# Four graph-attention layers on one core: another engine order for the last blocks of two layers, and a residual addition moved from VectorE to TensorE and ScalarE

## The chip, the core and the metric

The kernel runs on one core of a Trainium2 chip. TensorE (PE, with its weight loads PEld), VectorE (DVE), ScalarE (ACT), GpSimd (POOL) and SyncE (SP) each work through a queue of their own, in order; semaphores hold an instruction until what it needs is done. Times are device microseconds (us) of one execution.

## The reference

4096 nodes with 256 features go through four attention layers over one sparse symmetric graph `adj` (about 9 neighbours to a node, itself among them). With `h = relu(layernorm(x))` each layer adds to the residual:

```
layer 0:  x += elu(softmax_over_neighbours(leaky(s_i + s_j)) @ Wh)        Wh = h W, 4 heads
layer 1:  x += h W + softmax_over_neighbours(leaky(s1_i + s2_j)) @ h      1 head
layer 2:  x += softmax_over_neighbours(leaky(s_i + s_j)) @ x',            x' = h W + b, 4 heads
layer 3:  x += softmax_over_neighbours(q k / 8) @ v                       4 heads
```

The text counts layers 0 to 3 as here; the change's "layers two and three" are layers 1 and 2.

## The kernel before

**Stages.** A scan reads the adjacency matrix, makes each node's list of up to 24 neighbours, sorts the nodes by degree into 32 blocks of 128, and does layer 0's first six neighbours of each node. Then `late` (L1122 to L1347) does what is left of layer 0 and makes layer 1's rows; `layer(1)`, `layer(2)` and `layer(3)` follow (L1349 to L1536). A block has between 3 and 23 slots for neighbours (`CAPS`), 15 of them at most are gathered one by one. For each slot GpSimd issues one indirect DMA (`fetch`, L1047, the call in L1048), which brings 128 rows, one per partition, from a table in DRAM into a ring in SBUF. The first gather of a layer needs every row of that layer's table, since any node may be anyone's neighbour.

**One block in a layer** passes through these stages, each a function inside `layer`:

- `scores` (L1538): the neighbours' scores on VectorE and ScalarE, and the exp on ScalarE; in layer 1 ScalarE adds the two halves of the score (L1550, L1551), and VectorE compares lists (L1608); in layer 2 VectorE adds them (L1553, L1554).
- `weigh` (L1615): VectorE makes the weights (L1627, L1628) and multiplies the gathered rows in the ring (L1654); TensorE sums the products over the slots with an identity matrix (L1634, L1662, L1668) in PSUM.
- `settle` (L1675): VectorE brings the new x out of PSUM (L1689) and takes its statistics (L960, L962); ScalarE turns them into scale and shift in a chain of eight tiny instructions (L965 to L972).
- `norm`: ScalarE makes h (L975), TensorE transposes it (L985).
- `flip`: ScalarE copies the transposed h to SBUF (L987).
- `product`: TensorE multiplies it with the next layer's weights (L1028).
- `third`: the product leaves PSUM, is stored to the next table by SP (L1712 in layer 1, L1730 in layer 2). In layer 1 ScalarE copies it (L1710), for the last two blocks VectorE adds the bias (L1708). In layer 2 VectorE adds biases to k and v (L1728) and q (L1732), then multiplies q with k and reduces (L1735, L1739), and ScalarE sums squares of q and k (L1742).

**What sets the order.** `manual_schedule` keeps the engines' instructions in program order, so the loop in `layer` is the order written out by hand. In step i it scores and weighs the i-th block of `ORDER`, and does the other stages for earlier blocks, by lags: S for settle, N for norm, Q for product, F for flip, T for third. `upto(name, k)` does a stage for all blocks up to k. Lags shrink over the last six steps. After the loop come the stages of what is left. TensorE's four PSUM banks are handed out by hand; `room` first does flips and thirds where too few are free. `told_by` makes a reader that comes in a later step than the product wait for the last sum of that step instead of for the product itself.

**The late part** goes over 19 groups of one or two blocks (`LATE`). `settle(i)` there is a generator of five steps: (0) ScalarE's exp of the sum, and minus 1 (L1287, L1288); (1) VectorE makes the new x (L1290, L1291) and its statistics; (2) scale and shift (L661 to L666), h on ScalarE (L1300), transposes on TensorE (L1307); (3) ScalarE copies them (L1310), and `times` (L1020) multiplies with layer 1's extended weights (L1028); (4) VectorE adds h W to x (L1317), ScalarE copies the scores' halves (L1318) and the list of neighbours (L1319) into the row, which GpSimd then sends to its place in the table (L1065). Each iteration does these for several groups:

```
scores(i)
go_on(i - 2)   # step 2
go_on(i - 1)   # step 0
go_on(i - 3)   # step 4
go_on(i - 2)   # step 3
weigh(i)
go_on(i - 1)   # step 1
```

Of the kernel before, what the change touches and what calls it, by code (L numbers as in the profile page):

```python
# [14 lines left out]
ALU = mybir.AluOpType  # L15
# [5 lines left out]
D = 256  # L21
# [30 lines left out]
W = 264  # L52
# [21 lines left out]
RAW = 6  # L74

AHEAD = 4

BOUND = 4900.0


class Sparse:
# [935 lines left out]
        self.wrote.append(m.ins)  # L1017
        self.latest = m.ins

    def times(self, ht, w, width, name, bias=None, ps=None):  # L1020
        if ps is None:
            ps = self.bank(f"s_ps_{name}")
        if bias is not None:
            self.writes(self.nc.tensor.matmul(
                ps[:, :width], lhsT=self.line, rhs=bias[0:1, :width], start=True, stop=False
            ))
        for c in range(KC):
            self.writes(self.nc.tensor.matmul(  # L1028
                ps[:, :width], lhsT=ht[:, c, :], rhs=w[:, c, :],
                start=(c == 0 and bias is None), stop=(c == KC - 1),  # L1030
            ))
        return ps[:, :width]

    def covered(self, g, start, size):
# [87 lines left out]
    def late(self):  # L1122


        nc, pool, nt, H = self.nc, self.pool, self.nt, 4
# [155 lines left out]
        def settle(i):  # L1281

            m, _ = size(i)
            xt, acc = part(i, 0, D), sums.pop(i)

            ex = pool.tile([P, 2, D], F32, name=f"s_ex_{i}", tag="ex", bufs=2)[:, :m, :]
            nc.scalar.activation(ex, acc, AF.Exp)  # L1287
            nc.scalar.activation(ex, ex, AF.Copy, bias=-1.0)  # L1288
            yield
            nc.vector.scalar_tensor_tensor(ex, ex, 0.0, xt, ALU.min, ALU.add)  # L1290
            nc.vector.scalar_tensor_tensor(xt, acc, 0.0, ex, ALU.max, ALU.add)  # L1291
            norm = self.norms_of(pool, xt if m > 1 else xt[:, 0, :], m, f"0_{i}", self.minus)
            for _ in range(m if m > 1 else 0):
                next(norm)
            next(norm)
            yield
            rn = next(norm)
            h = part(i, D, 2 * D)
            for u in range(m):
                nc.scalar.activation(  # L1300
                    h[:, u, :], xt[:, u, :], AF.Relu,
                    bias=rn[:, m + u : m + u + 1], scale=rn[:, u : u + 1],
                )
            pt = self.pp.tile([P, IB], F32, tag="ps", name=f"s_pht_0_{i}")
            for u in range(m):
                for c in range(KC):
                    nc.tensor.transpose(pt[:, ts(KC * u + c, P)], h[:, u, ts(c, P)], self.ident)  # L1307
            yield
            ht = pool.tile([P, 2, KC, P], F32, name=f"s_ht_0_{i}", tag="ht0", bufs=2)
            nc.scalar.copy(  # L1310
                ht[:, :m], pt[:, : m * KC * P].rearrange("p (n c r) -> p n c r", n=m, c=KC)
            )
            ps = [self.times(ht[:, u], self.we1, W, f"1_{i}_{u}") for u in range(m)]
            yield
            first = LATE[i][0]
            for u in range(m):
                nc.vector.tensor_tensor(xt[:, u, :], xt[:, u, :], ps[u][:, 0:D], ALU.add)  # L1317
                nc.scalar.copy(part(i, 2 * D, D + W)[:, u, :], ps[u][:, D:W])  # L1318
            nc.scalar.copy(part(i, D + W, D + WL), self.near[:, first : first + m, 0:TOPK])  # L1319
            pending.extend(LATE[i])  # L1320
            yield

# [26 lines left out]
    def layer(self, l):  # L1349
# [124 lines left out]
        def third(d):  # L1474
            if l < 3:
                step, wrote = when["row", d]
                self.reads = []
                next(rows.pop(d), None)
                if step < now:
                    for i in self.reads:  # L1480
                        told_by(i, wrote, step)
            while made and (len(made) > 1 or todo == []):
                i = self.send(*made.pop(0)).ins
                next_in_line(i)
                self.tc.declare_no_dep(i, group="results", reason="places differ")
                self.tc.add_to_no_dep_group("results", i)

        stages = {"settle": settle, "norm": norm, "flip": flip, "product": product, "third": third}
        done = {name: 0 for name in stages}

        def upto(name, k):
# [1 line left out]
                stages[name](ORDER[done[name]])  # L1493
                done[name] += 1

        for i in range(nt):
            now = i
            left = nt - 1 - i
            if l == 3:
                S = 1 if left < 3 else 2  # L1500
                N = F = Q = S + 1
                T = N
            else:
                S = 1 if left < 5 else 2
                N = 2 if left < 4 else 3
                Q = 2 if left < 2 else 3 if left < 4 else 4 if left < 6 else 5
                F, T = max(N, Q - 1), Q + 1
            fill(i)
            if (l, i) == (2, 4):
                self.symmetric()  # L1510
            b = ORDER[i]
            upto("norm", i - N)
            upto("product", i - Q)
            g = ring[:, held[b][0] : held[b][1], :]
            p = self.scores(l, b, self.rows[b], g)
            if l == 3:
                upto("third", i - T)
            sums[b] = self.weigh(l, b, vs.pop(b) if l == 3 else self.rows[b][:, 0:D], g, p)
            start, end = held.pop(b)
            past.append((start * wide, end * wide, self.read))  # L1520
            self.ever.append((start * wide, end * wide, self.read[0]))
            if l < 3:
                signals[i] = self.read[1]
            upto("settle", i - S)
            if l < 3:
                upto("flip", i - F)
                upto("third", i - T)
        now = nt
        upto("norm", nt - 2)
        upto("third", nt - 3)  # L1530
        upto("product", nt - 2)
        upto("settle", nt - 1)
        upto("norm", nt - 1)
        upto("third", nt - 2)
        upto("product", nt - 1)
        upto("third", nt - 1)  # L1536

    def scores(self, l, b, mine, g):  # L1538

# [155 lines left out]
    def advance(self, l, b, ht, made):  # L1695

        nc, pool = self.nc, self.pool
        xt = self.x[b]
        name = f"{l}_{b}"
        mine = self.rows[b]  # L1700
        if l == 2:
            short = b in ORDER[-2:]
            ps = self.times(ht, self.we2, W, name, None if short else self.be2)
            of_row = self.lent
            yield
            self.give(of_row)
            if short:
                i = nc.vector.tensor_tensor(mine, ps, self.be2, ALU.add)  # L1708
            else:
                i = nc.scalar.copy(mine, ps)  # L1710
            self.reads.append(i.ins)
            nc.sync.dma_start(out=self.tab[2][ts(b, P), :], in_=mine)  # L1712
        else:
            ps = self.times(ht, self.wkv, 2 * D, f"kv{name}")
            of_kv = self.lent
            spot, self.spot = self.spot, None
            if spot is not None and self.owed.get(spot[1]) == 1:
                of_q, spot = spot[1], spot[0]
# [9 lines left out]
            i = nc.vector.tensor_tensor(kv, ps, self.bqkv[:, D:], ALU.add)  # L1728
            self.reads.append(i.ins)
            nc.sync.dma_start(out=self.tab[3][ts(b, P), :], in_=kv)  # L1730
            q = mine[:, 0:D]
            i = nc.vector.tensor_tensor(q, ps_q, self.bqkv[:, 0:D], ALU.add)  # L1732
            self.reads.append(i.ins)
            qk = pool.tile([P, 4, 64], F32, name=f"s_qk_{b}", tag="qk", bufs=2)
            nc.vector.tensor_tensor(  # L1735
                qk, q.rearrange("p (h d) -> p h d", h=4),
                kv[:, 0:D].rearrange("p (h d) -> p h d", h=4), ALU.mult,
            )
            nc.vector.tensor_reduce(self.eself[:, b, :], qk, AX.X, ALU.add)  # L1739
            for k, v in ((0, q), (1, kv[:, 0:D])):  # L1740
# [580 lines left out]
```

## Time and profile before

| what | value |
|---|---|
| median of 15 runs | 1672.92 us (1665.64 to 1677.36) |
| profiled execution, its own time | 1673.05 us |
| its span, first to last instruction | 1671.3 us |
| granted TensorE clock, mean | 0.832 |
| busy: POOL, DVE, PE, ACT | 1142.2, 1109.1, 1078.3, 536.4 us |
| first gather of the late part, of layers 1, 2, 3 | 363.11, 543.06, 907.41, 1280.75 us |

A line of the timeline has the start, the duration, the engine and line, what it writes and reads with shapes, and in brackets how long the engine stood before it and what ended that. "issue" is time for which the profile shows no wait. A line of the waits has who waited for whom, the us in total, how often, and the longest. In a group's line of the page, the numbers behind the bar are busy us, the mean in ns, and the idle time before. A matrix product in 32-bit floats appears as two instructions.

### The profile page before, as it was taken

The page shows a single profiled execution, that of the slowest core. Times are in us where ns is not written, and L with a number is a line of the kernel's source. Part 1 is how long each engine was busy: PE and PEld are TensorE (multiplying, and loading weights), DVE is VectorE, ACT ScalarE, POOL GpSimd, SP SyncE. Part 2 cuts the span into 40 slices and gives each one's busy share as a digit, 9 for nine tenths or more (in the row PEclk, how much of TensorE's full clock was granted, in tenths as well). Part 3 has the DMA queues.
Part 4 walks back from the last instruction along what each step waited for, and adds up shares of the span by engine and source line. Part 5 has one row for each costly group of instructions (what it writes and reads, how often), then busy time and mean ns, then how long its engine had stood idle before and what let it go on. Part 6 is the DMA issues. An engine that isn't in the chain of part 4 may idle for free.

```text
span 1671.3 us, 14041 instructions
## 1 busy us (share of the span) xinstructions
PE 1078.3 (65%) x3179; PEld 584.6 (35%) x3179; DVE 1109.1 (66%) x2651; ACT 536.4 (32%) x1754; POOL 1142.2 (68%) x1241
## 2 busy tenths in 40 slices
PE   5857877605776357777784478778794455545555
PEld 4423333203443133444343234444452222322233
DVE  6669899816885255455552456676774797788787
ACT  6867664103344023333343023334342000000000
POOL 1267777767774777777772777777762777777775
PEclk9969989956897677898897689999998678777778
DMA  7899999466551444444442435444542776767664
GB/s 271 303 396 394 355 394 326 146 223 164 156 165 63 115 119 127 132 131 130 133 137 64 109 107 146 138 133 138 143 129 90 211 221 204 215 202 211 203 209 144
DMA packets 125908, 309.07 MB, mean 185 GB/s; under 512 B 35028, under 2 KB 53463, under 8 KB 125816
## 3 DMA queue, kind: packets, MB, share of 16 engines
q0 software_dynamic: 66832, 203.64, 41.8%
q1 hardware_dynamic: 58984, 104.46, 17.7%
q8 instruction: 27, 0.44, 0.1%
q14 instruction: 65, 0.53, 0.1%
HBM read 273.00 MB, written 35.00 MB: 184 GB/s over the span
## 4 chain that ended last, share of the span: by engine, by line
POOL 28%; DMA 22%; DVE 19%; issue 16%; ACT 9%; PE 6%; DVEq 0%; SPq 0%; POOLq 0%; ACTq 0%
POOL s_ring L1048 23%; DMA s_raw<-in_adj_dram 10%; DMA s_ring<-s_tab,s_near 10%; DVE s_ring L1654 5%; ACT s_low L277 2%; POOL s_placed L722 2%; POOL s_g L1048 1%; DVE s_ring L1575 1%; PE s_bank L1028 1%; DVE s_e L1579 1%; PE s_acc L1662 1%; POOL out_dram L1065 1%; DVE s_rx L1689 1%; DVE s_me L1639 1%; PE s_ps_t L1028 1%
## 5 line engine op out<-in xcount | busy, mean ns | idle before, releaser
L1048 POOL DMA_INDIRECT s_ring<-s_tab,s_near x900 | 855.7, 951 | 339.6 <-issue 266.6
L1662 PE MATMUL s_acc<-s_ring,s_ident 128*128 128x512 f32 (+1 forms) x1002 | 466.4, 623 | 273.3 <-DVE s_ring L1654 272.7
L1662 PEld LDWEIGHTS s_acc<-s_ring,s_ident 128*128 128x128 f32 x1002 | 225.5, 233 | 491.8 <-DVE s_ring L1654 305.0
L1048 POOL DMA_INDIRECT s_g<-s_tab,s_keep x192 | 182.8, 952 | 129.3 <-DMA s_raw<-in_adj_dram 65.5
L1654 DVE TENSOR_TENSOR s_ring<-s_ring,s_shares 128x2048 f32<-128x2048 f32 (+1 forms) x153 | 232.8, 1552 | 0.0
L277 ACT ACTIVATE s_low<-s_raw 128x1024 fp8e4<-128x1024 int32 x128 | 135.1, 1056 | 63.8 <-DMA s_raw<-in_adj_dram 62.3
L1600 ACT ACTIVATE s_shares<-s_e 128x40 f32<-128x40 f32 (+7 forms) x64 | 13.1, 205 | 332.4 <-DVE s_e L1597 332.4
L520 PE MATMUL s_pt<-s_low,s_mark_True 128*128 128x512 fp8e4 x256 | 83.6, 407 | 55.9 <-DVE s_cand L532 47.5
L1575 DVE TENSOR_TENSOR s_ring<-s_ring,s_shares 128x2048 f32<-128x2048 f32 (+7 forms) x47 | 78.8, 1676 | 55.9 <-DMA s_ring<-s_tab,s_near 38.8
L965 ACT ACTIVATE s_y<-s_mv,s_eps 128x1 f32<-128x1 f32 x64 | 18.8, 294 | 276.1 <-DVE s_mv L962 250.0
L532 DVE MAX8 s_cand<-s_pt 128x8 f32<-128x256 f32 x256 | 93.1, 415 | 13.8 <-PE s_pt L530 13.8
L1608 DVE TENSOR_SCALAR s_eq<-s_ring,s_own_f 128x207 bf16<-128x207 f32 (+12 forms) x32 | 12.5, 390 | 129.4 <-DMA s_ring<-s_tab,s_near 129.1
L631 PE MATMUL s_ae<-s_g,s_ident 128*128 128x512 f32 x192 | 90.8, 602 | 3.9 <-DVE s_g L622 3.9
L1579 DVE TENSOR_REDUCE s_e<-s_ring 128x32 f32<-128x2048 f32 (+7 forms) x47 | 78.9, 1679 | 1.6
L1028 PE MATMUL s_bank<-s_wkv,s_ht 128*128 128x512 f32 x128 | 62.9, 615 | 2.4 <-ACT s_ht L987 2.3
L520 PEld LDWEIGHTS <-s_mark_True 128*128 128x128 bf16 x256 | 23.3, 101 | 108.2 <-issue 61.4
L1028 PE MATMUL s_ps<-s_we_l,s_ht 128*128 128x264 f32 x128 | 45.0, 506 | 23.9 <-ACT s_ht L1310 23.9
L1634 PE MATMUL s_acc<-s_rx,s_ident 128*128 128x256 f32 x192 | 59.5, 393 | 0.0
L1307 PE MATMUL s_pht<-s_ident,s_rx 128*128 128x128 f32 x64 | 13.8, 325 | 69.1 <-DMA s_ring<-s_tab,s_near 50.8
L1668 PE MATMUL s_acc<-s_me,s_ident 128*128 128x256 f32 x192 | 57.1, 379 | 0.0
L622 DVE TENSOR_TENSOR s_g<-s_g,s_pe 128x1536 f32<-128x1536 f32 x32 | 55.4, 1735 | 0.0
L924 PE MATMUL s_bank<-s_to,s_to_row 128*128 128x32 f32 (+1 forms) x6 | 1.8, 393 | 81.4 <-DVE s_to L918 81.4
(286 smaller groups left out, 1830.6 us busy)
## 6 DMA issues: line engine op xcount, KB each, us to landing
s_raw<-in_adj_dram SPq DMA_DIRECT2D x128, 512.0 KB, 9.6
s_ring<-s_tab,s_near POOLq DMA_INDIRECT x900, 3.0
s_rx<-s_placed SPq DMA_DIRECT2D x32, 262.0 KB, 3.2
s_tab<-s_kv SPq DMA_DIRECT2D x32, 256.0 KB, 2.5
s_tab<-s_rx SPq DMA_DIRECT2D x32, 132.0 KB, 1.9
s_keep<-in_x_dram SPq DMA_DIRECT2D x8, 512.0 KB, 8.2
s_vself<-s_tab SPq DMA_DIRECT2D x32, 128.0 KB, 3.4
s_tab<-s_keep SPq DMA_DIRECT2D x7, 528.0 KB, 3.7
```

Of the source, the lines that this page charges most:

```text
L277: nc.scalar.activation(low[r][:, quarter(q)], raw.pop(q), AF.Copy, saturate=False, accum_out=self.sums[:, r, h : h + 1],)
L520: nc.tensor.matmul(pt, lhsT=self.mark[k], rhs=lo[:, k * PAIR + g * IB : k * PAIR + (g + 1) * IB], start=(k == 0), stop=False,)
L532: nc.vector.max(out=cand[:, g * (IB // CH) + k, :], in_=pt[:, ts(k, CH)])
L631: self.behind(got, nc.tensor.matmul(acc, lhsT=self.ident, rhs=g[:, :, k, 0:D], start=False, stop=(k == E - 1)))
L1028: self.writes(self.nc.tensor.matmul(ps[:, :width], lhsT=ht[:, c, :], rhs=w[:, c, :], start=(c == 0 and bias is None), stop=(c == KC - 1),))
L1048: return self.nc.gpsimd.indirect_dma_start(out=out, out_offset=None, in_=table[:, :], in_offset=bass.IndirectOffsetOnAxis(ap=idx, axis=0),)
L1575: scaled = nc.vector.tensor_tensor(kq, kq, q.unsqueeze(1).to_broadcast([P, m, D]), ALU.mult)
L1579: nc.vector.tensor_reduce(e[:, k0 : k0 + m, :], kq.rearrange("p k (h d) -> p k h d", h=4), AX.X, ALU.add)
L1634: self.took_x[b] = nc.tensor.matmul(acc[:, 1, :], lhsT=self.ident, rhs=self.x[b], start=True, stop=False)
L1654: scaled = nc.vector.tensor_tensor(v, v, p[:, k0 : k0 + m, :].unsqueeze(3).to_broadcast([P, m, H, D // H]), ALU.mult)
L1662: self.behind(self.got.get((l, b), ()), nc.tensor.matmul(acc[:, 0:n, :], lhsT=self.ident, rhs=g[:, k : k + n, v0 : v0 + D], start=False, s ...
L1668: last = nc.tensor.matmul(acc[:, 0, :], lhsT=self.ident, rhs=mev, start=False, stop=True).ins
```

## The change

Two edits that share nothing.

**The late part.** `times` gets an argument `also`: between the two halves of a row's product TensorE adds one more product, identity times x, into the first 256 columns of the same PSUM bank. VectorE's addition (L1317) goes. ScalarE copies those columns to x, after the copies L1318 and L1319 that complete the row for the table.

**The layers 1 and 2.** The lags come from a list: they shrink from the tenth block before the end on. The last four blocks have an order of their own: two of them are settled and norm'ed right behind their own sum; in the last step the block before is settled between scores and weights. In layer 2 the part of `third` behind the q addition becomes a stage `rest`, which runs later. Layer 3's own order stays what it was.

```diff
+SHORT = 4
+LAGS = [(1, 2, 2), (1, 2, 3), (1, 2, 3), (1, 2, 4), (1, 3, 4), (2, 3, 5)]
...
-    def times(self, ht, w, width, name, bias=None, ps=None):
+    def times(self, ht, w, width, name, bias=None, ps=None, also=None):
...
+            if c == 0 and also is not None:
+                self.took = self.nc.tensor.matmul(
+                    ps[:, 0:D], lhsT=self.ident, rhs=also, start=False, stop=False
+                ).ins
...
-            ps = [self.times(ht[:, u], self.we1, W, f"1_{i}_{u}") for u in range(m)]
+            ps, took = [], []
+            for u in range(m):
+                ps.append(self.times(ht[:, u], self.we1, W, f"1_{i}_{u}", also=xt[:, u, :]))
+                took.append(self.took)
             yield
             first = LATE[i][0]
             for u in range(m):
-                nc.vector.tensor_tensor(xt[:, u, :], xt[:, u, :], ps[u][:, 0:D], ALU.add)
                 nc.scalar.copy(part(i, 2 * D, D + W)[:, u, :], ps[u][:, D:W])
             nc.scalar.copy(part(i, D + W, D + WL), self.near[:, first : first + m, 0:TOPK])
+            for u in range(m):
+                c = nc.scalar.copy(xt[:, u, :], ps[u][:, 0:D])
...
+        def shape(i):
+            upto("norm", i)
+            upto("flip", i)
+            upto("product", i)
...
-                S = 1 if left < 5 else 2
-                N = 2 if left < 4 else 3
-                Q = 2 if left < 2 else 3 if left < 4 else 4 if left < 6 else 5
-                F, T = max(N, Q - 1), Q + 1
...
+            elif left >= SHORT:
+                S, N, Q = LAGS[min(left - SHORT, len(LAGS) - 1)]
+                F, T = max(N, Q - 1), Q + 1
+                upto("norm", i - N)
+                upto("product", i - Q)
+                score(i)
+                weigh(i)
+                upto("settle", i - S)
                 upto("flip", i - F)
                 upto("third", i - T)
+                upto("rest", i - T)
+            elif left > 0:
+                upto("norm", i - 2)
+                upto("product", i - 2)
+                score(i)
+                upto("settle", i - 1)
+                upto("flip", done["norm"] - 1)
+                weigh(i)
+                shape(i - 1)
+                upto("third", i - 2)
+                if left > 1:
+                    upto("settle", i)
+                    upto("norm", i)
+                upto("rest", i - 3)
+            else:
+                score(i)
+                upto("settle", i - 1)
+                weigh(i)
+                upto("third", i - 2)
+                upto("rest", i - 3)
+                shape(i - 1)
+                upto("settle", i)
+                upto("norm", i)
+                upto("third", i - 1)
+                shape(i)
+                upto("third", i)
+                upto("rest", i)
...
             i = nc.vector.tensor_tensor(q, ps_q, self.bqkv[:, 0:D], ALU.add)
             self.reads.append(i.ins)
+            yield
             qk = pool.tile([P, 4, 64], F32, name=f"s_qk_{b}", tag="qk", bufs=2)
```

The stages in program order over the last five steps, before and after, in layer 2 (numbers are places in `ORDER`; thirds and flips that `room` brings forward stand where they run):

```
before  27: norm24 product23 SCORE27 WEIGH27 settle25 settle26 flip24 third22
        28: norm25 norm26 flip25 flip26 third23 product24 product25 SCORE28 WEIGH28 settle27 third24
        29: norm27 product26 SCORE29 WEIGH29 settle28 flip27 third25
        30: norm28 product27 flip28 third26 third27 product28 SCORE30 WEIGH30 settle29
        31: norm29 flip29 product29 SCORE31 WEIGH31 settle30 third28
       end: norm30 third29 flip30 product30 settle31 norm31 third30 flip31 product31 third31
after   27: norm25 product24 flip25 third23 third24 product25 SCORE27 WEIGH27 settle26 rest23 rest24
        28: norm26 flip26 product26 SCORE28 settle27 WEIGH28 third25 third26 norm27 flip27 product27 settle28 norm28 rest25
        29: SCORE29 flip28 WEIGH29 product28 third27 settle29 norm29 rest26
        30: SCORE30 flip29 WEIGH30 product29 third28 rest27
        31: SCORE31 settle30 WEIGH31 third29 rest28 norm30 flip30 product30 settle31 norm31 third30 flip31 product31 third31 rest29 rest30 rest31
```

In layer 1 the order after is the same without the rests, with third23 and third24 behind settle26 and with third25 and third26 behind product27.

More of the change, by code (lines that the diff above doesn't have):

```diff
@@ L1316, in settle @@
             for u in range(m):
-                nc.vector.tensor_tensor(xt[:, u, :], xt[:, u, :], ps[u][:, 0:D], ALU.add)
                 nc.scalar.copy(part(i, 2 * D, D + W)[:, u, :], ps[u][:, D:W])
             nc.scalar.copy(part(i, D + W, D + WL), self.near[:, first : first + m, 0:TOPK])
+            for u in range(m):
+                c = nc.scalar.copy(xt[:, u, :], ps[u][:, 0:D])
+                self.tc.declare_no_dep(c.ins, took[u], reason="the row's last product is waited for")
             pending.extend(LATE[i])
@@ L1477, in third @@
                 self.reads = []
-                next(rows.pop(d), None)
+                next(rows[d], None)
                 if step < now:
@@ L1486, in third, with rest @@
                 self.tc.add_to_no_dep_group("results", i)
-        stages = {"settle": settle, "norm": norm, "flip": flip, "product": product, "third": third}
+        def rest(d):
+            next(rows.pop(d), None)
+        stages = {
+            "settle": settle, "norm": norm, "flip": flip, "product": product, "third": third,
+            "rest": rest,
+        }
         done = {name: 0 for name in stages}
@@ L1494, in upto, with score, weigh @@
                 done[name] += 1
[L1496 to L1503, printed above, removed]
-                S = 1 if left < 5 else 2
-                N = 2 if left < 4 else 3
-                Q = 2 if left < 2 else 3 if left < 4 else 4 if left < 6 else 5
-                F, T = max(N, Q - 1), Q + 1
-            fill(i)
-            if (l, i) == (2, 4):
-                self.symmetric()
-            b = ORDER[i]
[L1512 to L1518, printed above, removed]
+        block = lambda i: ring[:, held[ORDER[i]][0] : held[ORDER[i]][1], :]
+        scored = {}
+        def score(i):
+            b = ORDER[i]
+            scored[i] = self.scores(l, b, self.rows[b], block(i))
+        now = 0
+        def weigh(i):
+            nonlocal now
+            b = ORDER[i]
+            me = vs.pop(b) if l == 3 else self.rows[b][:, 0:D]
+            sums[b] = self.weigh(l, b, me, block(i), scored.pop(i))
             start, end = held.pop(b)
@@ L1522, in layer @@
             if l < 3:
-                signals[i] = self.read[1]
-            upto("settle", i - S)
-            if l < 3:
+                signals[i], now = self.read[1], i + 1
+        def shape(i):
+            upto("norm", i)
+            upto("flip", i)
+            upto("product", i)
+        for i in range(nt):
+            left = nt - 1 - i
+            fill(i)
+            if (l, i) == (2, 4):
+                self.symmetric()
+            if l == 3:
+                S = 1 if left < 3 else 2
+                score(i)
+                upto("third", i - S - 1)
+                weigh(i)
[7 more added lines that the diff above has]
+                weigh(i)
+                upto("settle", i - S)
                 upto("flip", i - F)
                 upto("third", i - T)
[L1528 to L1536, printed above, removed]
+                upto("rest", i - T)
[13 more added lines that the diff above has]
+            else:
+                score(i)
+                upto("settle", i - 1)
+                weigh(i)
+                upto("third", i - 2)
[7 more added lines that the diff above has]
+                upto("rest", i)
+        if l == 3:
+            upto("third", nt - 3)
+            upto("settle", nt - 1)
+            upto("third", nt - 1)
     def scores(self, l, b, mine, g):
```

## The prediction

> **What bounds the kernel now.** I read the page's groups first. The dearest line is GpSimd's gather, one instruction per neighbour slot:
>
> ```profile
> L1048 POOL DMA_INDIRECT s_ring<-s_tab,s_near x900 | 855.7, 951 | 339.6 <-issue 266.6
> ```
>
> 951 ns and 0.30 us of issue make 1.25 us each. Then GpSimd's timeline, for where that rhythm breaks between layers:
>
> ```profile
> 538.29 0.97 POOL L1065 DMA_INDIRECT s_tab<-s_rx,s_near  x1 [3.67 <-ACT s_rx L1319]
> ...
> 543.06 0.98 POOL L1048 DMA_INDIRECT s_ring<-s_tab,s_near  x1 [2.53 <-issue]
> ...
> 907.41 0.94 POOL L1048 DMA_INDIRECT s_ring<-s_tab,s_near  x1 [26.78 <-issue]
> ...
> 1280.75 0.94 POOL L1048 DMA_INDIRECT s_ring<-s_tab,s_near  x1 [34.99 <-PE s_bank L1767]
> ```
>
> Layers 1 and 2 gather 270 slots each: 270 x 1.25 = 337.5 us, and 543.06 to 907.41 is that plus the pause of 26.8; in layer 2 the pause is 35.0. So outside the scan (which the change doesn't touch) the end is set by four things: when the late part's last row is sent (538.29), the two pauses, and layer 3, which starts at 1280.75 and whose work stays as it is. I read the engines' timelines in the late part and before each pause. What moves the first gather of the next layer moves the end by as much.
>
> **The late part.** Iteration i runs, in program order on each engine: scores(i); h(i-2); exp(i-1); rows out(i-3); the copy of h transposed and the product (i-2); weighted sum(i); norm(i-1). One iteration on ScalarE, then TensorE, then VectorE:
>
> ```profile
> 497.46 0.60 ACT L1310 COPY s_ht<-s_pht 128x512 f32<-128x512 f32 x1
> ...
> 502.77 0.60 ACT L1287 ACTIVATE s_ex<-s_acc 128x512 f32<-128x512 f32 x1 [0.51 <-PE s_acc L1272]
> 503.40 0.63 ACT L1288 ACTIVATE s_ex<-s_ex 128x512 f32<-128x512 f32 x1
> ...
> 504.17 0.38 ACT L1310 COPY s_ht<-s_pht 128x256 f32<-128x256 f32 x1
> ```
>
> ```profile
> 498.11 2.05 PE L1028 MATMUL s_ps<-s_we_l,s_ht 128*128 128x264 f32 x8 [1.22 <-ACT s_ht L1310]
> ...
> 500.85 1.88 PE L1272 MATMUL s_acc<-s_ring,s_ident 128*128 128x512 f32 x4
> ```
>
> ```profile
> 501.54 0.74 DVE L1317 TENSOR_TENSOR s_rx<-s_rx,s_ps 128x256 f32<-128x256 f32 x2
> ...
> 504.94 0.68 DVE L1290 SCALAR_TENSOR_TENSOR s_ex<-s_ex,s_rx 128x512 f32<-128x512 f32 x1
> ```
>
> Read them as a ring: copy (497.46), product (498.11), sum (to 502.73), exp (502.77), minus 1, small copies, next copy (504.17): 6.7 us with nothing idle in it. VectorE's own iteration (499.85 to 507.54, with 0.5 idle) is as long. Two rings are level. The change takes 0.74 (two rows; 0.41 for one) from VectorE's and puts work into the other:
> - TensorE: one more identity product of 256 columns per row, between the two halves. Nearest row: L1634, the same shape, whose pair of instructions (0.59) lets the next start 0.43 later. 0.43 a row.
> - ScalarE: one 128x256 copy out of PSUM per row, queued ahead of the next block's copy L1310. Nearest row: L987, 0.65 for two in a row, 0.36 for one.
>
> From iteration 5 (413.5, where computing is 16 us behind the gathers) to 18 the ring gets 22 products (9.5) and copies of 8 pairs and 6 single blocks (8 x 0.65 + 6 x 0.36 = 7.4): +16.9. Slack in it: ScalarE found the sum ready before it came to exp in four iterations (0.65, 0.15, 2.4, 2.0) and 0.3 in the last, 5.5 in all. +11.4. The last group has its two products at the slow pitch of 533.27 (3.88 for 8): +1.8, less the 0.42 addition that its rows no longer wait for: +1.4. Sum **+12.8**. GpSimd covers none of it: from 512 on its sends wait for ScalarE (L1319). The new copies stand behind L1319, so no row's own send waits for them.
> Ends: the clock. The same 8 instructions take 2.05 at 521.08 and 3.6 to 3.9 at 450.18, 491.08, 512.32, 533.27, after gaps. If busier TensorE keeps the short time at all four, 4 x 1.6 go: +6. If the added products always ran at the long pitch (0.9): 22 x 0.45 more would be +22, which the gaps at only four places make unlikely. Below nothing: if VectorE alone were the ring, six iterations x 0.74, -4.5; against it the waits below. I take **+10**, nearer to the rows at 498 and 521 than to those after gaps.
>
> ```profile
> ACT s_ex L1287 <- PE s_acc L1272: 12.2, 9, 3.4
> DVE s_ex L1290 <- ACT s_ex L1288: 11.2, 5, 3.9
> ```
>
> In nine iterations ScalarE stood for TensorE's sum, in five VectorE then stood for ScalarE.
> The clock's rows, 2.05 against 3.6 to 3.9, bear on a rule that speaks for this change: the Trainium skill, "TensorE: Matmul & The Clock Gate", Part 1, has the array at half rate until a window of about 3.4 us was busy. By it the added products would help to keep the rate, and the late part would cost +6 rather than +12.8. Another speaks against it: "ScalarE: Activation LUTs", Rules for kernel authors, wants additions on VectorE rather than ScalarE. By the rows ScalarE's 0.36 replaces VectorE's 0.41, so by length the move costs nothing; the cost lies in the queue.
>
> **The end of layer 1.** Before, block 28 of the order is scored at 859.92, 29 and 30 as soon as their rows land, 31 four us late:
>
> ```profile
> 868.86 0.32 DVE L1608 TENSOR_SCALAR s_eq<-s_ring,s_own_f 128x184 bf16<-128x184 f32 x1 [0.39 <-DMA s_ring<-s_tab,s_near]
> ...
> 878.79 0.32 DVE L1608 TENSOR_SCALAR s_eq<-s_ring,s_own_f 128x184 bf16<-128x184 f32 x1 [2.16 <-DMA s_ring<-s_tab,s_near]
> ...
> 886.25 0.29 DVE L1608 TENSOR_SCALAR s_eq<-s_ring,s_own_f 128x69 bf16<-128x69 f32 x1
> ...
> 895.33 0.69 DVE L1689 TENSOR_REDUCE s_rx<-s_acc 128x256 f32<-128x512 f32 x1 [0.84 <-PE s_acc L1668]
> ```
>
> The new order settles and norms blocks 28 and 29 right behind their own sums, and the next score stands behind that on VectorE and ScalarE. The sum of 28 ends at 872.9 as before. Then: settle and statistics 1.4, ScalarE's chain 1.9, h 0.5, so ScalarE comes to 29's scores at 876.7 (870.9 before); from there to the end of its sum 8.6 (the rows 870.92 to 879.5): 885.3. Again 3.8, then 2.1 to the first product and 4.7 to the sum of 30: 895.9. The rows of 28 leave PSUM behind that sum (the code waits for the step's last sum), and 31's scores behind them: 896.4, its products at 899.4, its sum at 902.4 (895.3 before). What follows took 12.1 before (895.3 to 907.4) and takes 10.0 now, because less is left over: settle 1.4, 0.4 behind 30's copy, chain 1.9, h 0.6, transposes and copy 0.9, product 1.2, addition 0.5, store to first gather 3.1. First gather at 912.4, +5. Ends: +1 if 28's rows are out before the sum of 30, +6 if the last product takes 2.1 as before (901.68). I take **+4**, between them: whether a wait falls there is read from the code alone.
>
> **The end of layer 2.** The same with 2 us more per step (VectorE's kv and q additions, ScalarE's squares), and here data waits already before:
>
> ```profile
> 1251.30 0.18 DVE L1554 TENSOR_TENSOR s_e<-s_ring,s_rx 128x32 f32<-128x32 f32 x1
> ...
> 1257.22 0.17 DVE L1554 TENSOR_TENSOR s_e<-s_ring,s_rx 128x12 f32<-128x12 f32 x1
> ...
> 1277.18 0.69 DVE L1728 TENSOR_TENSOR s_kv<-s_bank,s_bqkv 128x512 f32<-128x512 f32 x1 [2.56 <-PE s_bank L1028]
> ```
>
> The rows of 30 and 31 had landed at about 1244 and 1248 (last gathers 1241.05 and 1244.81, 3.0 to land). A step in which two blocks are norm'ed or multiplied took 15.0 (first weighting 1194.87 to 1209.85), 13.5 and 14.2; a plain one 7.6 to 8.4; rows come every 8.8 to 11.3. The old lags have the three double steps at 26, 28, 30; the new ones at 23, 24, 25, 27, and then the special steps. A double step now is 14.3 (sum 8.2, transposes 0.45, product and q addition 3.3, scores and weights 2.3); step 24, two h's without a second product, 12.4; 26, plain, but with the squares of two blocks, 9.5. With 14.3, 12.4, 14.3, 9.5, 14.3 from 1163.84 block 27 is weighted at 1228.6 (1217.4 before). To the sum of 28 18.6: products 2.3, settle 1.4, chain 1.9, squares 2.2, h 0.5, turned 0.8, weights 1.3, products 2.3, rest of the sum 5.9 (20.4 before). To that of 29 13.7: rows of 26 out 1.1, settle 1.4, chain 1.9, h 0.5, squares 1.1, weights 1.2, products 2.3, rest 4.2. To that of 30 11.9 (products in pairs), of 31 8.1 (rows of 28 and rest 1.9, scores 1.0, settle 1.4, weights 1.0, sum 2.8). To the first gather 12.3: rows of 29 out and rest 1.9, settle 1.4, chain 1.9, h 0.6, turned 0.9, kv 1.9, addition 0.7, store 2.9 (15.0 before: the squares of 30 stood ahead of 31's copy). 1293: +12. If only step 27 is late (block 26 on time at 1205.3), block 27 is at 1219.3: +3. I take **+8**, the middle, since both rest on the same rows. Moving "rest" behind the stores costs nothing: after 1281 VectorE stands 11.6 us for layer 3's first rows; SP has only these stores to issue.
>
> **Sum.** 10 + 4 + 8 = +22 on the profiled 1673.05 (span 1671.3; its time is 0.1 from the median, 1672.92): **1695**.
>
> **Rivals.**
> - *The tails pay for themselves* (20%): the leftover that goes in the last step (2.1 and 2.7) and a shorter queue at 23 to 27 cancel the waits; only the late part stays: 1673 + 6 to 12, 1682. For it: before, 31's scores wait for ScalarE from 886.8 to 890.6 and from 1258.0 to 1260.8.
> - *Faster* (13%): the ring between the sum of one block and of the next in steps 28 to 30. I price it at 11 to 13.7 against 10 of gathering. Below 10 the scores are not late any more, 31 starts at its rows' landing: 4 and 8 us come back in the two pauses, and if VectorE was the late part's bound, 4.5 there: -12, 1661.
> - *It cancels* (9%): late part +6, both tails -3: within 0.2%.
> - Forecast, all three slower: 58%, 1686 to 1706.
>
> Within 0.2% (3.3 us) is what a measurement of this kernel can't tell from no change: 9%; faster 13%, slower 78%. The range leaves out the faster case and a small part above: from 1672 (cancelled) to 1706 (the upper ends 12.8 + 6 + 12 = 31, rounded up).
>
> **What would show it.** Right: last send of the late part at 546 to 552, more waits of L1287 for L1272, VectorE idle in the late part; pauses of 30 to 31 and over 40 us; scores 29 and 30 of layer 1 standing for ScalarE and no longer for the DMA. Wrong: a late part that ends by 538, its 8-instruction products all near 2.1; pauses under 26.8 and 35.0; the last four scores starting as rows land.

## The result, and the profile after

The changed kernel takes **1706.72 us** (median of 8 runs, 1704.14 to 1714.39; before in the same comparison 1671.88, 40 runs). The ratio is 1.0214, 95% interval 1.02 to 1.0228: 34.8 us slower. The forecast was 1695 in a range of 1672 to 1706, so the sign was right and the time lies 0.7 us outside the range. The profiled run took 1707.31 us with a span of 1705.6.

GpSimd's timeline again, where its rhythm breaks (in the new line numbers L1071 sends a row, L1054 gathers):

```profile
545.67 0.97 POOL L1071 DMA_INDIRECT s_tab<-s_rx,s_near  x1 [2.08 <-ACT s_rx L1327]
...
550.44 0.98 POOL L1054 DMA_INDIRECT s_ring<-s_tab,s_near  x1 [2.53 <-issue]
...
924.94 0.94 POOL L1054 DMA_INDIRECT s_ring<-s_tab,s_near  x1 [37.20 <-issue]
...
1311.31 0.94 POOL L1054 DMA_INDIRECT s_ring<-s_tab,s_near  x1 [48.20 <-DVE s_qk L1789]
```

Set against before, the loss falls in four places (their sum is 35.3, the spans differ by 34.3; some tenths come back elsewhere):

| place | before | after | difference |
|---|---|---|---|
| first gather of the late part to that of layer 1 | 179.95 | 187.94 | +8.0 |
| pause ahead of layer 2 | 26.78 | 37.20 | +10.4 |
| pause ahead of layer 3 | 34.99 | 48.20 | +13.2 |
| first gather of layer 3 to the end of the span | 390.55 | 394.3 | +3.7 |

The late part in the view of waits (who stood, for whom, us in total, times, longest). Before, the three lines had 23.9, 12.2 and 11.2 (the first is shown with the late half's experiments, the others in the prediction):

```profile
PE s_ps L1030 <- ACT s_ht L1316: 33.1, 19, 2.2
ACT s_ex L1293 <- PE s_acc L1278: 30.7, 12, 5.6
DVE s_ex L1296 <- ACT s_ex L1294: 28.6, 12, 6.7
```

The ring is longer, and VectorE, which lost its additions, only waits more. Three views of the end of layer 1. VectorE's timeline first (L1742 settles, L1661 compares for the next scores):

```profile
881.62 0.69 DVE L1742 TENSOR_REDUCE s_rx<-s_acc 128x256 f32<-128x512 f32 x1 [6.03 <-PE s_acc L1721]
883.18 0.32 DVE L1661 TENSOR_SCALAR s_eq<-s_ring,s_own_f 128x184 bf16<-128x184 f32 x1 [0.20 <-DMA s_ring<-s_tab,s_near]
...
895.94 0.69 DVE L1742 TENSOR_REDUCE s_rx<-s_acc 128x256 f32<-128x512 f32 x1 [6.08 <-PE s_acc L1721]
897.50 0.32 DVE L1661 TENSOR_SCALAR s_eq<-s_ring,s_own_f 128x184 bf16<-128x184 f32 x1 [0.19 <-issue]
```

VectorE stands 6 us for the sum of 28 and then of 29, settles it, and only then comes to the scores of 29 and 30. ScalarE's timeline (L1763 copies rows out of PSUM, L1603 begins the scores):

```profile
895.94 0.38 ACT L1763 COPY s_rx<-s_bank 128x264 f32<-128x264 f32 x1 [8.88 <-PE s_acc L1721]
...
899.76 0.29 ACT L1603 ACTIVATE s_e<-s_ring,s_rx 128x8 f32<-128x8 f32 x1
...
909.12 0.38 ACT L1763 COPY s_rx<-s_bank 128x264 f32<-128x264 f32 x1 [7.74 <-PE s_acc L1721]
909.39 0.30 ACT L1603 ACTIVATE s_e<-s_ring,s_rx 128x3 f32<-128x3 f32 x1
```

It stands 8.9 and 7.7 us with a finished row for the step's last sum, and the scores of 31 are queued right behind. TensorE's timeline, the slots' products in the sums of 29 and 30:

```profile
889.91 5.55 PE L1715 MATMUL s_acc<-s_ring,s_ident 128*128 128x256 f32 x10 [3.46 <-DVE s_ring L1707]
...
902.64 6.01 PE L1715 MATMUL s_acc<-s_ring,s_ident 128*128 128x256 f32 x10 [1.72 <-DVE s_ring L1707]
```

The same ten instructions took 3.71 and 3.60 before, when TensorE had not stood ahead of them:

```profile
875.40 3.71 PE L1662 MATMUL s_acc<-s_ring,s_ident 128*128 128x256 f32 x10
...
883.79 3.60 PE L1662 MATMUL s_acc<-s_ring,s_ident 128*128 128x256 f32 x10
```

Layer 3 is the one place where nothing was foreseen. In five profiled runs of the experiments, on chips that take the same time for the kernel before, the stretch is 389.5 to 392.4 us, with either half of the change in; the 3.7 us show in the one run above alone, and what they are stays open.

### The profile page after: what moved, and what is told of

It is laid out like the page before. It is cut to its first block, busy times and chain, and to the rows that moved or that the text cites. A ratio compares the mean times of both kernels' runs of the same rounds, so it can differ in the third digit from the quotient of the medians.

```text
span 1705.6 us, 14167 instructions
## 1 busy us (share of the span) xinstructions
PE 1096.0 (64%) x3243; PEld 598.4 (35%) x3243; DVE 1096.9 (64%) x2619; ACT 545.5 (32%) x1786; POOL 1141.0 (67%) x1241
## 4 chain that ended last, share of the span: by engine, by line
POOL 27%; DMA 20%; issue 18%; DVE 15%; PE 10%; ACT 9%; DVEq 0%; POOLq 0%; SPq 0%; ACTq 0%
POOL s_ring L1054 22%; DMA s_raw<-in_adj_dram 9%; DMA s_ring<-s_tab,s_near 9%; DVE s_ring L1707 5%; PE s_acc L1715 3%; PE s_acc L1278 2%; POOL s_g L1054 2%; ACT s_low L279 2%; POOL s_placed L724 2%; PE s_ps L1030 2%; DVE s_ring L1628 1%; DVE s_e L1632 1%; POOL out_dram L1071 1%; DVE s_rx L1742 1%; PE s_ps_t L1030 1%
## 5 line engine op out<-in xcount | busy, mean ns | idle before, releaser
L1054 POOL DMA_INDIRECT s_ring<-s_tab,s_near x900 | 854.3, 949 | 363.3 <-issue 279.5
L1715 PE MATMUL s_acc<-s_ring,s_ident 128*128 128x512 f32 (+1 forms) x1002 | 472.8, 631 | 286.1 <-DVE s_ring L1707 285.9
L1054 POOL DMA_INDIRECT s_g<-s_tab,s_keep x192 | 183.2, 954 | 128.6 <-DMA s_raw<-in_adj_dram 64.9
L1661 DVE TENSOR_SCALAR s_eq<-s_ring,s_own_f 128x207 bf16<-128x207 f32 (+12 forms) x32 | 12.3, 385 | 118.0 <-DMA s_ring<-s_tab,s_near 117.3
L1071 POOL DMA_INDIRECT s_tab<-s_rx,s_near x32 | 32.5, 1014 | 35.3 <-ACT s_rx L1327 21.8
L987 PE MATMUL s_bank<-s_ident,s_h 128*128 128x128 f32 x128 | 26.6, 290 | 45.1 <-ACT s_h L977 44.9
```

What stands on the lines that cost most here:

```text
L1054: return self.nc.gpsimd.indirect_dma_start(out=out, out_offset=None, in_=table[:, :], in_offset=bass.IndirectOffsetOnAxis(ap=idx, axis=0),)
L1715: self.behind(self.got.get((l, b), ()), nc.tensor.matmul(acc[:, 0:n, :], lhsT=self.ident, rhs=g[:, k : k + n, v0 : v0 + D], start=False, s ...
```

## The experiments

Two kinds of chip have to be told apart here. Five runs fell on two chips that take 1673 to 1675 us for the kernel before; the others on four chips that take 1981 to 1998 (one of them 1981.7 in one comparison and 1998.4 in another). No chip showed both kinds. On the second kind there are long stretches in which TensorE's instructions come far apart (shown in the last section), so a time there says something only beside another from the same comparison.

### Each half alone

Late half only: the hunks on `times` and the late `settle`. Layers' half only: all the others.

> The late part's edit alone, layers 1 to 3 as before. Theory (the rows' extra product and copy lengthen the ring of ScalarE, TensorE and ScalarE): the first gather of layer 1 at about 550.4 instead of 543.1, the pauses ahead of layers 2 and 3 as before (26.8 and 35.0), so about 8 us more than before, 1680. Rival (VectorE was the bound of the late part, and the 8 us of the changed kernel are something else's): 4.5 us less, 1668. If layer 3's 3.7 us more belong to this edit, they show here as well.

1682.81 us, ratio 1.0059 (1.0046 to 1.0072), +9.9 on the medians. First gather to first gather the late part takes 188.38, +8.4; the pauses are 27.89 and 33.61. The first theory holds, the rival is out.

> The order of layers 1 and 2 alone, the late part as before. Theory (two edits that share nothing): the pauses ahead of layers 2 and 3 as in the changed kernel, 37 and 48, so 10.4 + 13.2 = 23.6 us more than before, 1696; with the 3.7 us of layer 3, if they come from this edit, 1699. Rival (the late edit shifts something that makes the tails dear): pauses under 32 and 40, less than 12 us more.

1701.87, ratio 1.0167 (1.0153 to 1.0181), +29.0. Pauses 36.84 and 54.03. The second is 5.8 longer than in the changed kernel: in this profile the last sum's six products take 2.93 instead of 1.56, and VectorE stands 6.19 instead of 4.51 for the last product behind it, 3.1 of the 5.8. So a pause read from one profile can differ by some us between two kernels with the same order. The halves add up to 38.9 against the 34.8 measured together; the two come from different comparisons, and I leave that difference open.

### The late half: which of the two added pieces

```diff
-            for u in range(m):
-                c = nc.scalar.copy(xt[:, u, :], ps[u][:, 0:D])
+            waiting.append(out)    # the copies, issued behind the next group's copy of h
```

> The late part's edit alone (9.9 us more than before when run by itself), but ScalarE copies a group's x out of PSUM only behind the next group's copy of the transposed h, so that this copy and the product behind it no longer wait for it. Theory (both added pieces stand in the ring of ScalarE's copy, TensorE's product and sum, and ScalarE's exp: 0.43 us of product and 0.36 of copy a row): the copies leave the ring, since ScalarE then stands for TensorE's sum anyway, and 4 to 6 of the 10 us come back: 1677 to 1679, with the first gather of layer 1 at about 545 to 547. Rival (only TensorE's extra products lengthen the ring, and the copies already lay beside them): within 2 us of the late edit alone.

1676.44, ratio 1.001 (1.0001 to 1.0019): nearly all of the loss is gone, more than the theory gave. The late part takes 182.21, +2.3 instead of +8.4. The waits of TensorE for the copy of h, with the late half alone:

```profile
PE s_ps L1028 <- ACT s_ht L1314: 32.9, 19, 2.2
```

and with the copies of x put behind:

```profile
PE s_ps L1028 <- ACT s_ht L1314: 24.7, 19, 1.7
```

8.2 us less, close to the line of before:

```profile
PE s_ps L1028 <- ACT s_ht L1310: 23.9, 19, 1.7
```

So about 6 of the 8.4 us are ScalarE's copies in front of the next copy of h. The 2.3 that are left are what TensorE's extra products, the addition that VectorE lost and TensorE's pitch come to together. No run takes these apart, and where the late part is left as it was, the stretch already spreads over 2.7 us (before 179.95; layers' order alone 177.54, lags alone 179.19, no settle behind the own sum 180.21). A faster pitch is not what makes the loss go here: of the four products that took 3.6 to 3.9 before (450.18, 491.08, 512.32, 533.27), the late half alone keeps one at the slow pitch (454.64 on its own clock), but the run with the copies behind keeps three, two of them in part (452.58, 515.45, 536.16).

### The layers' half: lags or last four

```diff
+                if left >= SHORT:
+                    S, N, Q = LAGS[min(left - SHORT, len(LAGS) - 1)]
```

This goes into the loop of before; the last four blocks keep their order.

> Layers 1 and 2 with the new lags down to the fifth block before the end, and the order of before for the last four blocks and behind the loop; late part as before. Theory (the loss is the ring of sum, settle, chain and next scores in the last four steps): the lags move work ahead and cost little, pauses of 26 to 28 and 35 to 39, 0 to 5 us more than before. Rival (the double steps that the lags bring forward to 23 to 27 in layer 2 are the loss): pause ahead of layer 3 of 43 or more, at least 8 us more.

1673.95, ratio 1.0006 (0.9996 to 1.0015): nothing that can be measured. Pauses 25.25 and 37.71. Counted from its layer's first gather, block 27 of layer 2 is weighted 9.9 us later than before (1224.80 less 904.88, against 1217.43 less 907.41), but block 31 only 3.0: most of the delay is made up in four blocks, and the rest is this pause's 2.7. So the loss comes in with the order of the last four blocks.

### The last four: settle behind the own sum

```diff
-                if left > 1:
-                    upto("settle", i)
-                    upto("norm", i)
```

> As the run of the layers' order alone, but blocks 28 and 29 are no longer settled and norm'ed right behind their own sums (they are settled in the next step, between or behind its scores and weights). Theory (that settle is what puts the next scores behind the sum): scores 29 and 30 start as their rows land or soon after, pauses of about 28 to 31 and 37 to 41, so 3 to 10 us more than before. Rival (the loss is in the rest of the new order, the rows that wait for the step's last sum and the products behind it): within 3 us of the run of the layers' order alone, 20 us or more above before.

1690.35, ratio 1.0104 (1.0089 to 1.0118): 11.5 us come back of 29.0, neither the 19 to 26 of the theory nor nothing. Pauses 32.59 and 45.36. VectorE's timeline in this kernel, layer 2 (L1769 brings k and v out of PSUM, L1595 begins the scores, L1730 settles):

```profile
1252.82 0.69 DVE L1769 TENSOR_TENSOR s_kv<-s_bank,s_bqkv 128x512 f32<-128x512 f32 x1 [4.65 <-PE s_acc L1709]
...
1254.62 0.18 DVE L1595 TENSOR_TENSOR s_e<-s_ring,s_rx 128x32 f32<-128x32 f32 x1
...
1265.91 0.69 DVE L1769 TENSOR_TENSOR s_kv<-s_bank,s_bqkv 128x512 f32<-128x512 f32 x1 [5.93 <-PE s_acc L1709]
...
1267.71 0.18 DVE L1595 TENSOR_TENSOR s_e<-s_ring,s_rx 128x32 f32<-128x32 f32 x1
```

The settle is gone from ahead of the scores, and the scores still start 1.8 us behind the sum: now the row that leaves PSUM waits for it. A row's product made behind one sum is read behind the next, and `told_by` lets it wait for that next sum. In layer 2, two separate things hold the same scores.

### The waits for the step's last sum

```diff
-                if step < now:
+                if step < now and now < nt - 3:
```

in `third` and `flip`: from behind the sum of 28 on, each reader waits for its own product. With the settle left in:

> The layers' order alone (29 us more than before when run by itself), but from behind the sum of block 28 on, the rows and the transposed copies that leave PSUM wait for their own products and no longer for the step's last sum. Theory A (most of the loss is the ring from a sum over its own settle to the next scores): the ring stays, only the 1.0 to 1.7 us per step go in which rows leave PSUM between a sum and its settle, and scores 31 of layer 1 need not wait for the sum of 30: 5 to 8 us less, 1694 to 1697. Theory B (the waits for the step's last sum, behind which the next scores stand in the queues of VectorE and ScalarE, are the loss): 15 us less or more, 1687 or below.

2015.98 against 1982.53, ratio 1.016 (1.0118 to 1.0202); once more on another of these chips 1.0167 (1.0133 to 1.0201). Neither theory's number can be read from these times. With the settle out as well:

> Both taken out of the layers' order: blocks 28 and 29 are not settled right behind their own sums (17.5 us more than before when run by itself), and rows and transposed copies wait for their own products. Theory (there are two ways in which the next scores come to stand behind a sum, the settle and the wait for the step's last sum, and taking out one leaves the other): scores 29 to 31 no longer wait for a sum, pauses near 26 and 36, within 5 us of before, 1670 to 1678. Rival (the wait for the step's last sum costs nothing, since what stands behind it would be late anyway): 1687 to 1691, as without this edit.

2004.54, ratio 1.0086 (1.0052 to 1.012); in three more comparisons on such chips 1.0109 (1.006 to 1.0158), 1.0136 (1.01 to 1.0171) and 1.0123 (1.0076 to 1.017). Within 5 us of before it is not, on these chips. To take the waits by themselves, two kernels side by side:

> No settle right behind the own sum, the waits for the step's last sum left in; a second time, so that it has the next run's chip. On a chip like the first 1690, on one that takes 1985 for the kernel before some 2005 to 2015.

> The same, and rows and transposed copies wait for their own products. Theory (with the settle gone, these waits still hold the next scores behind a sum): 8 us or more below the run beside it, and pauses shorter by that. Rival (what stands behind the waits would be late anyway): within 3 us of it.

2018.61, 1.0185 (1.0136 to 1.0235), with the waits; 2005.49, 1.0105 (1.0073 to 1.0137), without: 13 us on the medians, with intervals that just touch. The two profiled executions do not show that difference as a whole (2018.30 with, 2024.18 without; pauses of 71.39 and 109.40 against 71.00 and 105.05). The view of waits shows what went, in the first

```profile
DVE s_kv L1769 <- PE s_acc L1709: 20.8, 7, 5.9
```

and in the second

```profile
DVE s_kv L1769 <- PE s_acc L1709: 8.8, 4, 3.3
```

The end of a layer can also be measured by itself. The table has the us on VectorE from the start of block 28's scores to the last row's addition out of PSUM:

| kernel | layer 1 | layer 2 |
|---|---|---|
| before | 43.9 | 48.5 |
| before with `rest` last (below), second kind of chip | 49.0 | 50.5 |
| changed kernel | 54.3 | 57.9 |
| layers' order alone | 53.8 | 62.5 |
| no settle behind the own sum | 49.7 | 52.2 |
| the same, second kind of chip | 53.1 | 52.2 |
| settle left in, own waits, second kind, two profiles | 55.6, 56.9 | 52.6, 52.5 |
| both taken out, second kind, five profiles | 51.9 to 54.6 | 41.6 to 42.8 |

In layer 2 the kernel without the settle takes 52.2 on both kinds of chip, so the column can be read across them, to about the 2 us between its first two rows. Either piece alone gives 5 to 10 us, both together 15 to 21. With both out (the second of the two kernels above) the scores no longer wait for a sum: VectorE begins them and stands for the sum only afterwards, at the settle:

```profile
1545.29 0.18 DVE L1595 TENSOR_TENSOR s_e<-s_ring,s_rx 128x32 f32<-128x32 f32 x1
...
1548.23 0.69 DVE L1730 TENSOR_REDUCE s_rx<-s_acc 128x256 f32<-128x512 f32 x1 [2.02 <-PE s_acc L1709]
```

That is the theory, for layer 2: 9.4 of the 13 us stand there. In layer 1 the waits gave nothing, and ScalarE's timeline of the same run shows a third piece (L989 copies the transposed h, L1591 is ScalarE's part of the scores):

```profile
1057.81 0.37 ACT L989 COPY s_ht<-s_bank 128x256 f32<-128x256 f32 x1 [6.94 <-PE s_bank L987]
...
1058.62 0.33 ACT L1591 ACTIVATE s_e<-s_ring,s_rx 128x8 f32<-128x8 f32 x1
```

The transposes (L987) of block 27 stand behind the sum of block 28 in TensorE's own queue, the copy of them stands ahead of the scores of 29 in ScalarE's, and in layer 1 ScalarE adds the scores' halves. No run took this third piece out, and none measured the two others' price in the time on a chip like that of the forecast; the lags' 1.1 and the settle's 11.5 leave 16.4 of the 29.0 us there for all the rest.

### TensorE's slow sums

```diff
+        if l < 3 and b in ORDER[-3:-1]:
+            for _ in range(6):
+                nc.tensor.matmul(acc[:, 1, :], lhsT=self.ident, rhs=self.x[b], start=True, stop=True)
```

A first trial wrote these products beside the weights in PSUM:

> The layers' order alone, and TensorE gets six more products of the same shape, whose result nothing reads, ahead of the sums of blocks 28, 29 and 30 in layers 1 and 2, where it would stand for VectorE. Theory (the sums of 29 and 30 take 5.4 to 6.4 us instead of 3.7 because TensorE stood 1.5 to 3.5 us before them): the four sums take 3.7 to 4.2, about 8 us less than the layers' order alone, 1694. Rival (the slow pitch comes from elsewhere): the sums stay at 5.4 or more, and the added products at a slow pitch put them later, 1702 or more.

2047.04, 1.0324 (1.0282 to 1.0366), slower than anything: VectorE's weights then waited for them, 7.8 us from the block's first product to the slots' instead of 4.0. The second trial is the diff above:

> The layers' order alone (1701.9 us), and six products more on TensorE ahead of the sums of blocks 29 and 30 in layers 1 and 2, written where the sum's own first product overwrites them, so that no other engine waits for them (in the first trial VectorE's weights waited for them: 7.8 us from the block's first product to the first slot's instead of 4.0). Theory (the sums of 29 and 30 are slow because TensorE stood before them): 3.7 to 4.2 us each instead of 5.4 to 6.4, about 8 us less, 1694. Rival (the pitch does not follow what TensorE did just before): sums of 5.4 or more, 1702 or more.

2014.41, 1.0171 (1.0129 to 1.0214) against 1981.71; on one more such chip 1.0204 (1.017 to 1.0238), beside 1.0167 for the kernel with its own waits. TensorE's timeline at the end of layer 1, with the added products (L1680) and the slots' (L1709), blocks 29 and 30:

```profile
1053.88 4.11 PE L1680 MATMUL s_acc<-s_rx,s_ident 128*128 128x256 f32 x12
...
1058.27 3.60 PE L1709 MATMUL s_acc<-s_ring,s_ident 128*128 128x256 f32 x10
...
1066.58 4.44 PE L1680 MATMUL s_acc<-s_rx,s_ident 128*128 128x256 f32 x12
...
1071.29 3.60 PE L1709 MATMUL s_acc<-s_ring,s_ident 128*128 128x256 f32 x10
```

and without them, in the kernel that has its own waits, also in layer 1 and on another such chip:

```profile
1061.08 6.48 PE L1706 MATMUL s_acc<-s_ring,s_ident 128*128 128x256 f32 x10 [2.79 <-DVE s_ring L1698]
...
1074.73 6.48 PE L1706 MATMUL s_acc<-s_ring,s_ident 128*128 128x256 f32 x10 [1.85 <-DVE s_ring L1698]
```

That these sums are slow because TensorE stood ahead of them is shown: in the two runs with the added products all eight sums of 29 and 30 take 3.60 to 3.71, in the two runs with own waits and without them 5.22 to 6.48. One run of each was on the same chip. What it is worth is less: in layer 1 the added products take the slow pitch upon themselves (4.11 and 4.44 for twelve; in layer 2 2.75 to 4.33) and the sum starts later by part of what it gains. From the last product of one sum to that of the next it is 12.9 and 13.0 us, against 14.3 and 13.2 in the changed kernel. No gain in the time could be shown; the stretch of the table above is 54.2 in layer 1, no shorter than without them.

### Two tries for a faster kernel

Scores of 31 first in the last step, and `rest` behind the last store, in the order of before:

```diff
+                score(i)
+                upto("norm", i - 2)
+                upto("flip", i - 2)
+                upto("product", i - 2)
+                weigh(i)
```

> The order of before, with two edits at the end of layers 1 and 2: in the last step the scores of 31 come first, ahead of the h and product of 29, and what follows the stores (q times k and the squares of the last three blocks) comes behind the last store. Late part as before. Theory (31's scores stood for ScalarE 3.8 and 2.8 us, and the squares of 30 stood ahead of 31's copy): pauses of about 24 and 31, 5 us less than before, 1668. Rival (the sum of 30 and the chain behind it end as late as now, whatever 31 does): within 2 us of before.

1991.43 against 1982.53, ratio 1.0041 (1.001 to 1.0072): slower. It isolates less than it should, since its loop also counts a step as over behind its sum, as the change does, so that copies of the same step wait for that sum. Then `rest` alone:

```diff
+            upto("third", nt - 1)
+            upto("rest", nt - 1)
```

> The kernel before, with one thing of the change: in layer 2 the products of q with k and the squares of blocks 29, 30 and 31 come behind the last store. Theory (the squares of block 30 stood ahead of 31's copy of the transposed h on ScalarE, 2.6 us from h to copy instead of 0.9): pause ahead of layer 3 of 32 to 33.5 instead of 35.0, 1670 to 1671. Rival (31's chain ends as late as now for another reason): 1673, pause 35.

1998.89 against 1998.44, ratio 1.001 (0.9979 to 1.0042): no difference, but the interval on that chip is wider than the 2 us in question. No version here beats the kernel before. Whether layer 2's end with both pieces out (41.6 to 42.8 against 48.5) would do so on a chip of the first kind was not tried.

## Why the prediction was right or wrong, step by step

- **Late part, +10: right in size, less so in its terms.** 8.0 in the changed kernel, 8.4 (9.9 on the medians) alone. The copies were counted at 7.4, and putting them out of the way gave back 6.1. Without them the forecast's sum is 9.5 of products less 5.5 of slack plus 1.4, that is 5.4; 2.3 was measured. The step down from 12.8 for the clock went the right way: three of the four slow products are fast in the changed kernel, though one that had been fast became slow (514.30). The rule that the prediction set against the rows (the Trainium skill, "TensorE: Matmul & The Clock Gate", Part 1: the faster rate comes after a busy window) points the way that this trace went, 0.84 of granted clock between 355 and 550 us against 0.77 before. The rival with VectorE as the bound is out: VectorE gave up 10 us of work, the late part still grew, and VectorE stood longer for ScalarE (28.6 against 11.2).
- **End of layer 1, +4: the term that failed most.** Measured +10.4. The hand sum was +5 and I took less. In the time of before (7.38 subtracted, the late part's) the sum of 28 ended at 874.2 (forecast 872.9), that of 29 at 888.5 (885.3), of 30 at 901.7 (895.9), of 31 at 907.5 (902.4), the gather came at 917.6 (912.4). The order of events is as forecast. The mis-sized terms are the slots' products of 29 and 30, counted at 3.7 and 3.6 and measured at 5.55 and 6.01, 4.3 us together. Another 1.3 come from the sum of 28, taken "as before": the new order puts the settle of 27 between 28's scores and weights. I had read the rows of sums that TensorE reached without a wait, though the new ring puts a wait ahead of each; and one page up I had priced just that for the late part.
- **End of layer 2, +8: the choice that failed.** The hand sum gave +12 and a first gather at 1293; measured in before's time, 1311.31 less 17.53, 1293.8. That it meets to a microsecond is partly luck: the sum of 28 ended 3.1 us earlier than summed (1244.1 against 1247.2), and the two steps behind it took 15.9 and 14.0 instead of 13.7 and 11.9, again with slow products (6.18 and 5.85). The "middle" stood on the case that only step 27 is late, with block 27 weighted at 1219.3. It was weighted at 1227.2; the hand sum had 1228.6. That the late block 27 is not what matters most is shown by the lags alone: it is 9.9 us late there as well, and the pause grows by 2.7, with the old order behind it. Block 27 and the ring are separate, and I had averaged over them.
- **What holds the scores: half seen.** The forecast named the settle in the last four steps, and the wait of rows for the step's last sum only for 31's scores in layer 1. In layer 2 the experiments show both at work, and taking out one leaves most of the other; in layer 1 the copy of the transposed h stands there too. In the time, taking out the settle leaves 17.5 of 29.
- **"Rest" behind the stores costs nothing: not contradicted.** From the end of the last k and v addition to the first gather it is 2.88 us before and after. The last line of the first view names a product of q with k (L1789) as what released the gather; that is the latest event ahead of it and not the cause, since the store's 2.88 us are unchanged.
- **Layer 3 unchanged:** +3.7 in one profile, not seen with either half alone; open.

With each hand sum taken as it stood, 12.8 + 5 + 12, the forecast would have been 1703, 4 us from the result. That nearness is luck in part: 12.8 is 4.8 too much for the late part, 5 is 5.4 too little for layer 1, and layer 3's 3.7 is in no sum. Three times I moved toward the milder end; in the late part that came nearer, at the ends of the layers the reason was weaker than the sum.

## What to carry to other kernels

Where an order written by hand lets an engine do something for block i right behind the sum of block i, read what stands behind it in that engine's queue: if it is the start of block i + 1, the pipeline has become a ring. Look for every instruction ahead of that start which waits for the sum, in each engine that takes part in it: they hide each other, and taking out one gives back less than all. An operation put ahead of a copy that another engine waits for cost most of its length here (6.1 of the 7.4 us counted); behind that copy little was left (+2.3 instead of +8.4).

## What the runs showed of the hardware

Ten equal instructions of TensorE, the slots' products of the late blocks, took 3.60 or 3.71 us in most cases where it came to them with a wait of at most 1.1 us. Behind waits of 2.8 to 3.8 us they took 5.2 to 6.5 every time. In between it went both ways: with the settle out, one sum took 3.71 after a wait of 1.70, and with the layers' order alone one took 5.97 after 1.69. What decides there is open.

Of the six chips of the experiments four took 1981 to 1998 us for the kernel before, with a granted clock of 0.76 to 0.77 as the mean over the span instead of 0.83. It isn't a slower pitch throughout: there are stretches in which TensorE gives out one instruction every 2.8 us, with no wait that the profile shows. From TensorE's timeline of the kernel that scores 31 first, on such a chip:

```profile
759.93 0.59 PE L1698 MATMUL s_acc<-s_ring,s_ident 128*128 128x512 f32 x1 [0.90 <-issue]
762.73 0.59 PE L1698 MATMUL s_acc<-s_ring,s_ident 128*128 128x512 f32 x1 [2.21 <-issue]
765.53 0.59 PE L1704 MATMUL s_acc<-s_me,s_ident 128*128 128x256 f32 x1 [2.21 <-issue]
```

In that stretch ScalarE stood 23.52 us ahead of its copy of the transposed h; the view names nothing on this core as what ended it. The granted clock was 0.68 between 752 and 784 us, and the pause ahead of layer 2 was 60.53 us, so there the gathers end long before the computing does. What holds TensorE back on these chips is open.
